# Output-projection pieces of a group-norm attention kernel regrouped: casts behind a block's last chain, stores and residual loads at a burst's head, chains of one tile evacuated together, last sums in two parts

## Chip, cores and metric

The kernel runs on one core of a Trainium2 chip. The metric is the device time of one execution in microseconds; it is compared by the median of several runs.

## What is computed

The input x has 4 batches of 512 channels with 48 x 48 = 2304 positions. Group normalisation over 32 groups is followed by a 1 x 1 convolution to q, k and v, attention in 8 heads of 64 channels over all 2304 positions, an output projection and the residual:

```
hn = group_norm(x, scale, bias)
qkv = einsum('oc,bct->bot', qkv_w, hn) + qkv_b          # 3 x 8 heads x 64, float16
w = softmax(einsum('bhct,bhcs->bhts', q*s, k*s))        # s = 64 ** -0.25
a = einsum('bhts,bhcs->bhct', w, v)
out = x + einsum('oc,bct->bot', proj_w, a) + proj_b
```

## The kernel before

**Tiling.** Channels lie in 4 chunks of 128 partitions, heads go in pairs, and the positions of queries are cut into 5 blocks: 0 to 3 of 512 columns, block 4 of 256. A *burst* is one step of the stream of attention work: three tiles `ps` of scores in PSUM (L924, a pair of heads side by side), three exponentials to `p` on ScalarE (L931), a running sum `acc` of them on VectorE (L978), and, two bursts later, three tiles' worth of products with v into `av` (L949). A full block takes 6 bursts, block 4 takes 3; with 16 pairs (4 batches x 4) there are 432 bursts. Scores, values and the opening's chains run in the pool `ps_s` (3 tiles of two PSUM banks each), `av` and the sums in `ps_av` (one bank), and all chains beside the stream in `ps_w` (one bank, `pw`).

**Beside the stream.** What the next pairs need is cut into pieces and put into a list `beside`: q and k chains (`qk_chain`, L709, evacuated by VectorE in L718), v chains (L754, L762), loading and normalising the next batch, and the output projection of the batch before. `fill(n)`, called once per burst, lets tasks run in a given room, raises a credit by the rate at which pieces come due (each piece has an estimated cost and a pair by which it must be done) and issues pieces from the head of the list as long as the credit is at least half of the piece's cost. Pieces have an earliest burst (`after`). A chain that starts is not joined by a second one in the same burst. The order on every engine is the order in which these Python calls are made; no scheduler changes it.

**Sums.** At a block's end `add_up` (L1000) multiplies `acc` with ones, VectorE copies the result (`slx`, L1013), SyncE's queue moves it (`sums<-slx`, L1016), VectorE inverts it (L1042), the queue writes it to memory and spreads it (`row<-inv` L1044, `ib<-row` L1054), and GpSimd multiplies (`att`, L1061). For the last two blocks, `divide_here` (L1020 to 1024) does it in place with a long reciprocal on VectorE.

**Output projection.** `att32` (L815 to 825) casts a block of `att` of up to four pairs on ScalarE to `a`; `proj_run` (L841) makes a chain of 8 matmuls (4 pairs, two parts of the weights, L831) in a bank; `evacuate` adds bias and residual on VectorE (L858, or L854 for a last part); `store` (L863) writes the result. `residual` (L793) loads the part of x to be added; its tiles `r` come from a pool of 4. `proj_piece` ties them together: it loads the residual of the next chain, makes its own chain, evacuates it, and puts the store into a list `loads` for the next burst. `do_tasks` (L1104), called by `fill`, runs what is due in `loads`, so stores and reloads stand in the middle of a burst, behind the block's sums and inversion. A cast is a piece of no cost, other small pieces cost 0.05.

**The last batch.** For blocks 2, 3 and 4 of the last batch the projection is made in two parts: `FIRST`, three pairs, during the last pair's bursts, and `LAST`, the last pair's own part, at the end. `ready` (L1130) tells how many bursts after a block's end its cast may stand. After the stream, the sums of the very last block are made in one go in the bank `pw` (36 matmuls), the sums are tested against limits (`fines`, `good`, `flag`), and the remaining chains run, each in a bank of `ps_s` of its own since `alone` is set again.

**The opening.** Before the stream, six chains (k of blocks 0 to 4, q of block 0) run side by side in the six banks of three `ps_s` tiles, channel chunk by channel chunk as the normalised chunks come; with the last chunk each is evacuated right after its own matmuls.

Of the kernel before, what the change touches and what calls it, by code (L numbers as in the profile page):

```python
# [12 lines left out]
F32 = mybir.dt.float32  # L13
# [13 lines left out]
P = 128  # L27
NC = C // P
# [5 lines left out]
BEHIND = 2  # L34
# [433 lines left out]
def fast_path(  # L468
# [226 lines left out]
    def qk_steps(g, part, j, bank=None):  # L695
        b, pr = divmod(g, NPAIR)
        o, n = QBLOCKS[j]
        pw = {0: bank}

        def one(c):  # L700
            if g not in qk:
                qk[g] = [
                    qkp.tile([P, T], F16, tag=a, name=f"{a}_{g}") for a in ("q", "k")
                ]
            if c == 0 and bank is None:
                pw[0] = chain_bank(f"pqk_{g}_{part}_{j}")
            w0 = part * C + pr * P
            for lo in (0, D):
                nc.tensor.matmul(  # L709
                    pw[0][lo : lo + D, :n],  # L710
                    wqkv[:, c, w0 + lo : w0 + lo + D],
                    hn[b, c, j],
                    start=(c == 0),
                    stop=(c == NC - 1),
                )
            if c == NC - 1:
                col = part * NPAIR + pr
                nc.vector.tensor_scalar(  # L718
                    qk[g][part][:, o : o + n],
                    pw[0][:, :n],  # L720
                    bqkv[:, col : col + 1],
                    SCALE,
                    ALU.add,
                    ALU.mult,
                )

        return one

# [137 lines left out]

    def proj_piece(b, j, chunks, pairs=range(NC), ahead=None):
        def run():
            if ahead is not None:
                ahead()  # L870
            evacuate, store = proj_run(b, j, chunks, pairs)
            evacuate()
            if pairs != FIRST:

                loads.append((now[0] + 1, store))

        return piece(QB / 290.0 * len(pairs) / NC, run, True, True)

    def proj_pieces(b, j):

        def ahead(k):
            if k < len(proj_list) and not in_two(b, proj_list[k][0]):
                residual(b, *proj_list[k])

        def begin():
            att32(b, j, LAST if in_two(b, j) else range(NC))
            if j == 0:
                ahead(0)  # L890

        pairs = LAST if in_two(b, j) else range(NC)
        chains = [
            proj_piece(b, j, chunks, pairs, lambda k=k: ahead(k + 1))
            for k, (jj, chunks) in enumerate(proj_list)
            if jj == j
        ]
        return [piece(0.0, begin)], chains

    av, acc, pts, avx, sums, rowd, ibs = {}, {}, {}, {}, {}, {}, {}

    stream = []
# [76 lines left out]
                nc.vector.tensor_tensor(t[:, 0], t[:, 0], t[:, r], ALU.add)  # L981
            acc[g, j] = [t[:, :1]]

    def add_up(g, j, bank=None):

        o, n = QBLOCKS[j]
        per = QB // n
        sl = bank
        if bank is None:
            sl = ps_av.tile([P, QB], F32, tag="av", name=f"sl_{g}_{j}")  # L990
        steps = [
            (t, r, a)
            for t in acc.pop((g, j))
            for r in range(t.shape[1])
            for a in range(per)
        ]
        for i, (t, r, a) in enumerate(steps):
            for h in range(2):
                lo = h * D
                nc.tensor.matmul(  # L1000
                    sl[lo : lo + D, :n],
                    ones16,
                    t[:, r, h, a * n : (a + 1) * n],
                    start=(i == 0),
                    stop=(i == len(steps) - 1),
                )
        return sl

    def rows(g, j, sl):
# [92 lines left out]
        normed[b, j, c] = now[0]  # L1102

    def do_tasks(room):  # L1104
        n = now[0]
        while loads and loads[0][0] <= n:
            loads.popleft()[1]()
        while tasks and tasks[0][0] <= n and room > 0:
            _, us, run = tasks.popleft()
            run()  # L1110
            room -= us
# [18 lines left out]
    def ready(b, j):  # L1130

        if b < B - 1:
            return BEHIND + 6
        return BEHIND + 5

    def put_convert(b, j):
        end = ends[((b + 1) * NPAIR - 1) * NQ + j]
# [16 lines left out]
    for b in range(B):  # L1154
# [20 lines left out]
        if b == B - 1:  # L1175
            put_qk(g + 3, 1)
            put_qk(g + 3, 0, range(NQ - 1))
            put_convert(old, 0)
            put_qk(g + 3, 0, (NQ - 1,))

            ahead = [
                (residual, b, j, chunks)
                for j in (NQ - 2, NQ - 3, NQ - 1)
                for jj, chunks in proj_list
                if jj == j
            ]
            for j in range(NQ):
                put_proj(old, j, ahead)
                if j + 1 < NQ:
                    put_convert(old, j + 1)  # L1190
                if j >= NQ - 2:

                    there = ends[(NG - 2) * NQ + j] + BEHIND + 6
                    put_run(att32, b, j, FIRST, after=there)
            put_first(b, NQ - 2)
            put_run(att32, b, NQ - 3, FIRST)
            put_first(b, NQ - 3)
            put_convert(b, 0)
            put_proj(b, 0)
            put_first(b, NQ - 1)  # L1200
            put_convert(b, 1)
            put_proj(b, 1)
            put_convert(b, NQ - 3)
            put_proj(b, NQ - 3)
            continue
# [38 lines left out]
    for c in range(NC):  # L1244

        for j in range(NQ):
            if j == 2:
                coefficients(0, (c,))
                norm_chunk(0, c)
            if c + 1 < NC:  # L1250
                stats(0, j, c + 1)
        if c + 1 < NC:
            aggregate(0, (c + 1,))
            group_scale(0, (c + 1,))
        for chain in chains:
            chain(c)
    for j in range(1, NQ):
        for p in qk_chain(0, 0, j):
            p[1]()
# [12 lines left out]
    def fill(n):  # L1272
# [1 line left out]

        now[0] = n
        idle = beside and beside[0][4] and not beside[0][4]()
        if ended(n - 1):
            room = 1.1 if idle else 0.0  # L1280
# [5 lines left out]
        rate, work = 0.0, 0.0  # L1286
        for us, _, _, _, _, _, need in beside:
            work += us
            left = min(need * per_pair, len(stream) - BEHIND) - n
            rate = max(rate, work / max(left, 1))  # L1290
        credit[0] = min(credit[0] + rate, 4.0)
        closed = False
        while beside:
            us, _, first, last, when, after, _ = beside[0]
            if after > n or (first and closed) or (when and not when()):
                break
            if credit[0] < us / 2:
                break
            issue()
            closed = closed or last  # L1300
# [19 lines left out]
        return stream[n][:2] if ended(n) and n not in soon else None  # L1320

    for n in range(end):
        summed = block_at(n - BEHIND - 1)
        if summed:
            rows(*summed, add_up(*summed))
# [34 lines left out]
        loads.popleft()[1]()  # L1360
    check_sums(g, NQ - 2)
    att32(b, NQ - 2, LAST)
    add(stream[-1])
    values(stream[-1])
    sl = add_up(g, j, small_bank("sl_last"))

    every = fine.shape[1] + n
    fines = work.tile([P, QB], F32, tag="rows", name="fines")[:, :every]
# [5 lines left out]
    nc.gpsimd.tensor_copy(fines[:, n:], fine)  # L1374
    divide_here(g, j, sl, av[0], nc.vector)
    att32(b, j, LAST)
    alone[0] = True
    while beside or loads:
        while loads:
            loads.popleft()[1]()  # L1380
# [75 lines left out]
```

## Time and profile before

| | us |
|---|---|
| median of 3 runs (lowest, highest) | 1635.6 (1634.31, 1636.46) |
| the profiled execution: its own time | 1636.04 |
| its span from first to last instruction | 1634.3 |
| TensorE matmul busy | 1586.6 |
| ScalarE busy | 1284.2 |
| VectorE busy | 1135.6 |
| GpSimd busy | 301.2 |
| idle before the first matmul | 12.3 |

The mean granted clock of TensorE is 0.996 of full speed. In the profile, engines are called PE (matmuls), PEld (weight loads), DVE (VectorE), ACT (ScalarE), POOL (GpSimd) and SP (the SyncE queue that issues nearly all DMAs). A name such as `pr<-a,whi` is output and inputs of an instruction, L831 its line in the listing above. In lists of waits the numbers are the total, how often, and the longest, in us. In a timeline a bracket tells how long the engine was idle ahead of the row and what ended that. Matmuls overlap: the end of each is modelled, so a gap is read from one end to the next start, while the pace is read from start to start.

### The profile page before, as it was taken

To read this page: it belongs to the slowest core of one execution; us is meant where nothing else is said; L and a number is where in the kernel's file an instruction comes from. 1 tells how busy PE (TensorE), PEld (TensorE's weight loads), DVE (VectorE), ACT (ScalarE), POOL (GpSimd) and SP (SyncE) were. 2 spreads that over 40 slices of the span, in tenths; PEclk is the share of its full clock that TensorE was granted. 3 is DMA by queue.
4 is the path that set the end of the run, shared out by engine and by line. 5 is a ranking of instruction groups with operands and counts; after the bars stand their busy time and mean duration, and the time that the engine had idled before them with its cause. 6 is when DMAs were issued, how large, how long until landed. Compare 5 with 4: busy or idle time off the path is not lost.

```text
span 1634.3 us, 28292 instructions
## 1 busy us (share of the span) xinstructions
PE 1586.6 (97%) x11500; PEld 696.5 (43%) x11500; DVE 1135.6 (69%) x1302; ACT 1284.2 (79%) x1398; POOL 301.2 (18%) x419
## 2 busy tenths in 40 slices
PE   6999999999999999999999999999999999999896
PEld 2533434443333534555333353455433334435444
DVE  6268668866676677886666667788666766666575
ACT  3077777888888888888887888897888888887784
POOL 1001112211121221212111121221211121211111
PEclk9999999999999999999999999999999999999999
DMA  6002021000000024511000001451100000015423
GB/s 219 1 14 64 13 59 28 18 14 11 14 18 14 15 62 130 140 47 37 14 13 13 14 18 39 140 154 43 37 14 17 15 11 14 18 40 174 114 72 119
DMA packets 94898, 82.11 MB, mean 50 GB/s; under 512 B 50852, under 2 KB 60964, under 8 KB 94756
## 3 DMA queue, kind: packets, MB, share of 16 engines
q1 hardware_dynamic: 92724, 78.35, 17.3%
q8 instruction: 92, 1.51, 0.4%
q10 hardware_dynamic: 1904, 1.84, 0.4%
q14 instruction: 50, 0.41, 0.1%
q0 software_dynamic: 128, 0.01, 0.0%
HBM read 60.70 MB, written 19.17 MB: 49 GB/s over the span
## 4 chain that ended last, share of the span: by engine, by line
PE 88%; DVE 4%; ACT 3%; DMA 3%; issue 1%; SPq 0%; DVEq 0%; ACTq 0%
PE pqk L709 29%; PE ps L924 18%; PE av L949 18%; PE pv L754 15%; PE pr L831 5%; ACT p L931 3%; DMA r<-x_dram 2%; PE ps L709 1%; DVE acc L978 1%; PE sl L1000 1%; DVE r L858 1%; ACT a L825 1%; DMA x<-x_dram 1%; DVE inv L1023 0%; DVE r L854 0%
## 5 line engine op out<-in xcount | busy, mean ns | idle before, releaser
L931 ACT ACTIVATE p<-ps 128x1024 f16<-128x1024 f32 x1296 | 1232.4, 1026 | 316.1 <-PE ps L924 315.5
L978 DVE TENSOR_TENSOR acc<-acc,p 128x3072 f16<-128x3072 f16 x270 | 482.8, 1788 | 71.0 <-ACT p L931 69.9
L709 PE MATMUL pqk<-x,wqkv 128*64 128x512 f32 (+1 forms) x2464 | 519.5, 551 | 0.5 <-DVE r L858 0.5
L924 PE MATMUL ps<-q,k 64*128 64x512 f16 (+1 forms) x2880 | 358.7, 358 | 5.9 <-ACT p L931 5.1
L949 PE MATMUL av<-p,v 128*64 128x512 f16 (+1 forms) x2880 | 361.5, 364 | 0.4 <-DVE slx L1013 0.3
L754 PE MATMUL pv<-wqkv,x 128*64 128x256 f32 x2304 | 268.8, 380 | 0.0
L709 PEld LDWEIGHTS pqk<-x,wqkv 128*64 128x64 f32 x2464 | 168.9, 137 | 224.5 <-issue 164.9
L1035 POOL TENSOR_SCALAR in<-sums 128x8 f32<-128x8 f32 (+1 forms) x158 | 110.5, 700 | 800.9 <-DMA sums<-slx 794.5
L924 PEld LDWEIGHTS <-k 64*128 64x128 f16 x2880 | 106.8, 94 | 285.5 <-issue 237.8
L949 PEld LDWEIGHTS <-v 128*64 128x64 f16 x2880 | 132.1, 109 | 212.0 <-issue 167.9
L1061 POOL TENSOR_TENSOR att<-avx,ib 128x512 f16<-128x512 f32 (+1 forms) x78 | 128.7, 1650 | 453.7 <-DMA ib<-row 404.1
L754 PEld LDWEIGHTS pv<-wqkv,x 128*64 128x64 f32 x2304 | 160.6, 137 | 92.4 <-DVE v L762 3.6
L978 DVE TENSOR_TENSOR acc<-p,p 128x3072 f16<-128x3072 f16 x79 | 139.8, 1770 | 0.0
L831 PE MATMUL pr<-a,whi 128*128 128x512 f32 (+1 forms) x312 | 123.5, 403 | 13.8 <-ACT a L825 7.3
L831 PE MATMUL pr<-a,wlo 128*128 128x512 f32 (+1 forms) x312 | 115.8, 377 | 0.0
L981 DVE TENSOR_TENSOR acc<-acc 128x1024 f16<-128x1024 f16 x156 | 109.3, 701 | 5.3
L718 DVE TENSOR_SCALAR q<-pqk,bqkv 128x512 f16<-128x512 f32 (+1 forms) x79 | 55.0, 696 | 83.6 <-PE pqk L709 83.2
L762 DVE TENSOR_TENSOR v<-pv,bv 128x512 f16<-128x512 f32 x72 | 49.8, 691 | 85.5 <-PE pv L754 85.3
L718 DVE TENSOR_SCALAR k<-pqk,bqkv 128x512 f16<-128x512 f32 (+1 forms) x75 | 52.2, 696 | 79.2 <-PE pqk L709 79.0
L858 DVE SCALAR_TENSOR_TENSOR r<-pr,bproj,r 128x512 f32<-128x512 f32 (+1 forms) x80 | 54.9, 695 | 65.7 <-PE pr L831 46.7
L958 DVE COPY avx<-av 128x512 f32<-128x512 f32 (+1 forms) x79 | 50.7, 641 | 65.2 <-PE av L949 65.0
L831 PEld LDWEIGHTS pr<-a,whi 128*128 128x128 f32 x312 | 59.1, 189 | 52.4 <-issue 15.4
(62 smaller groups left out, 448.7 us busy)
## 6 DMA issues: line engine op xcount, KB each, us to landing
r<-x_dram SPq DMA_DIRECT2D x72, 256.0 KB, 3.4
out_dram<-r SPq DMA_DIRECT2D x69, 256.0 KB, 2.3
ib<-row SPq DMA_DIRECT2D x126, 128.0 KB, 3.0
x<-x_dram SPq DMA_DIRECT2D x62, 256.0 KB, 4.2
x<-x_dram SPq DMA_DIRECT2D x16, 128.0 KB, 3.8
sums<-slx SPq DMA_DIRECT2D x128, 2.0 KB, 2.1
ib<-row SPq DMA_DIRECT2D x30, 64.0 KB, 2.9
wqkv<-qkv_wT_dram SPq DMA_DIRECT2D x2, 768.0 KB, 6.9
```

Of the source, the lines that this page charges most:

```text
L709: nc.tensor.matmul(pw[0][lo : lo + D, :n], wqkv[:, c, w0 + lo : w0 + lo + D], hn[b, c, j], start=(c == 0), stop=(c == NC - 1),)
L718: nc.vector.tensor_scalar(qk[g][part][:, o : o + n], pw[0][:, :n], bqkv[:, col : col + 1], SCALE, ALU.add, ALU.mult,)
L754: nc.tensor.matmul(pw[0][lo : lo + D, a, :], hn[b, c, i * P // QB][:, at + lo : at + lo + D], wqkv[:, c, 2 * C + half * C // 2 :][:, : C / ...
L831: nc.tensor.matmul(ps[:, :n], w[:, c, bass.ts(m, P)], at32[b, j, c], start=(i == 0), stop=(i == len(steps) - 1),)
L858: nc.vector.scalar_tensor_tensor(xt[:, i], places[i], bias, xt[:, i], ALU.add, ALU.add)
L924: nc.tensor.matmul(ps[:, h, a * n : (a + 1) * n], kt[rows, bass.ts(i, P)], qt[rows, o : o + n], start=True, stop=True,)
L931: nc.scalar.activation(pt[:, r], ps, AF.Exp)
L949: nc.tensor.matmul(av[0][lo : lo + D, :n], vv[b, pr // 2][:, i, pr % 2 * P + lo : pr % 2 * P + lo + D], pt[:, r, h, a * n : (a + 1) * n], ...
L978: nc.vector.tensor_tensor(t, before, pt, ALU.add)
L981: nc.vector.tensor_tensor(t[:, 0], t[:, 0], t[:, r], ALU.add)
L1035: nc.gpsimd.tensor_scalar(t, sm, limit, None, op)
L1061: nc.gpsimd.tensor_tensor(atts[g][:, o : o + n], avx.pop((g, j))[:, :n], ibs.pop((g, j))[:, :n], ALU.mult,)
```

## The change

1. `qk_steps` returns its evacuation where a bank is given; the opening evacuates chains by twos, after both halves of a tile are written.
2. `proj_piece` makes its chain first and puts both its store and the residual load of the chain after the next into `loads`; the first two residuals are loaded with the block's cast. `loads` is now run at the head of each burst, ahead of the sums and scores, no longer in `do_tasks`.
3. A piece of cost up to 0.1 is issued whatever the credit, so a cast follows right behind the chain before it.
4. The last batch's order of FIRST parts and casts is rewritten; the cast of block 2's LAST part may stand one burst earlier; the rate towards the end of the stream is reckoned to 4 bursts before the end instead of 2.
5. The last sums are made in two parts in a `ps_s` tile, the first before the last values; `alone` is not set again, so chains left over after the stream share `pw`.

```diff
@@ qk_steps
-            if c == NC - 1:
+            def evacuate():
                 col = part * NPAIR + pr
                 nc.vector.tensor_scalar(
...
+            if bank is not None:
+                return evacuate
+            if c == NC - 1:
+                evacuate()
@@ proj_piece
         def run():
-            if ahead is not None:
-                ahead()
             evacuate, store = proj_run(b, j, chunks, pairs)
             evacuate()
             if pairs != FIRST:
                 loads.append((now[0] + 1, store))
+            if ahead is not None:
+                loads.append((now[0] + 1, ahead))
@@ proj_pieces
             if j == 0:
                 ahead(0)
+                ahead(1)
...
-            proj_piece(b, j, chunks, pairs, lambda k=k: ahead(k + 1))
+            proj_piece(b, j, chunks, pairs, lambda k=k: ahead(k + 2))
@@ add_up
-    def add_up(g, j, bank=None):
+    def add_up(g, j, bank=None, more=False):
...
-                    start=(i == 0),
-                    stop=(i == len(steps) - 1),
+                    start=(i == 0 and (g, j) not in open_sums),
+                    stop=(i == len(steps) - 1 and not more),
                 )
+        if more:
+            acc[g, j] = []
+            open_sums.add((g, j))
@@ do_tasks
-        n = now[0]
-        while loads and loads[0][0] <= n:
-            loads.popleft()[1]()
-        while tasks and tasks[0][0] <= n and room > 0:
+        while tasks and tasks[0][0] <= now[0] and room > 0:
@@ ready
-        return BEHIND + 5
+        return BEHIND + (4 if j == NQ - 3 else 5)
@@ the last batch
-                if j >= NQ - 2:
-                    there = ends[(NG - 2) * NQ + j] + BEHIND + 6
-                    put_run(att32, b, j, FIRST, after=there)
-            put_first(b, NQ - 2)
-            put_run(att32, b, NQ - 3, FIRST)
-            put_first(b, NQ - 3)
+            for j in (NQ - 2, NQ - 3, NQ - 1):
+                there = ends[(NG - 2) * NQ + j] + BEHIND + 6
+                put_run(att32, b, j, FIRST, after=there)
+                put_first(b, j)
             put_convert(b, 0)
             put_proj(b, 0)
-            put_first(b, NQ - 1)
@@ the opening
-        for chain in chains:
-            chain(c)
+        for i, chain in enumerate(chains):
+            evacuate = chain(c)
+            if c == NC - 1 and i % 2 == 1:
+                before()
+                evacuate()
+            before = evacuate
@@ fill
-            left = min(need * per_pair, len(stream) - BEHIND) - n
+            left = min(need * per_pair, len(stream) - 4) - n
...
-            if credit[0] < us / 2:
+            if us > 0.1 and credit[0] < us / 2:
@@ the stream
     for n in range(end):
+        now[0] = n
+        while loads and loads[0][0] <= n:
+            loads.popleft()[1]()
@@ the end
     att32(b, NQ - 2, LAST)
+    sl = ps_s.tile([P, 2, QB], F32, tag="ps", name="sl_last")[:, 0, :]
+    add_up(g, j, sl, more=True)
     add(stream[-1])
     values(stream[-1])
-    sl = add_up(g, j, small_bank("sl_last"))
+    add_up(g, j, sl)
...
-    alone[0] = True
```

More of the change, by code (lines that the diff above doesn't have):

```diff
@@ L898, in proj_pieces @@
         return [piece(0.0, begin)], chains
+    open_sums = set()
     av, acc, pts, avx, sums, rowd, ibs = {}, {}, {}, {}, {}, {}, {}
@@ L1272, in fill @@
     def fill(n):
-        now[0] = n
         idle = beside and beside[0][4] and not beside[0][4]()
```

## The prediction

> **What bounds the kernel now.** I read the page first: busy shares, the slices, the chain that ended last. TensorE (PE) is busy almost throughout, and the change leaves every matmul in place, so only time in which PE waits, or runs slowed, can be won. The first line gives busy time, share and instructions per engine.
>
> ```profile
> PE 1586.6 (97%) x11500; PEld 696.5 (43%) x11500; DVE 1135.6 (69%) x1302; ACT 1284.2 (79%) x1398; POOL 301.2 (18%) x419
> ```
>
> So 1634.3 - 1586.6 = 47.7 us without a matmul: 12.3 before the first, 8.7 after the last, and gaps between. The waits of PE name what ended each gap (total, times, longest):
>
> ```profile
> PE pr L831 <- ACT a L825: 7.3, 3, 3.0
> PE pr L831 <- DVE r L858: 6.1, 8, 1.7
> PE ps L924 <- ACT p L931: 5.1, 12, 0.5
> PE ps L709 <- DVE k L718: 2.7, 3, 0.9
> ```
>
> All four are places that the diff touches: output chains (L831) waiting for the converted att (L825) or for the previous chain's evacuation (L858), scores (L924) waiting for exponentials (L931), and the opening chains (L709) waiting for evacuations (L718). In the PE timeline of the opening the bracket is idle time ahead of a row:
>
> ```profile
> 27.81 1.88 PE L709 MATMUL ps<-x,wqkv 128*64 128x512 f32 x8
> 30.64 1.94 PE L709 MATMUL ps<-x,wqkv 128*64 128x512 f32 x8 [0.95 <-DVE k L718]
> 33.52 1.51 PE L709 MATMUL ps<-x,wqkv 128*64 128x512 f32 x8 [0.94 <-DVE k L718]
> 35.83 1.08 PE L709 MATMUL ps<-x,wqkv 128*64 128x512 f32 x4 [0.80 <-DVE k L718]
> 36.74 1.46 PE L709 MATMUL pqk<-x,wqkv 128*64 128x512 f32 x6
> ```
>
> Last the chain of waits in the last batch (start, duration, what): the path leaves PE for ACT's casts, and the chain of 8 matmuls after that takes 3.63 and 2.85 us where its neighbours take 2.07.
>
> ```profile
> 1498.08 0.47 ACT p L931
> 1498.55 0.45 issue
> 1499.00 1.94 ACT p L931 x2
> 1500.94 0.51 ACT a L825
> 1501.45 0.04 issue
> 1501.49 3.63 PE pr L831 x8
> ...
> 1517.11 2.85 ACT p L931 x3
> 1519.97 0.51 ACT a L825
> 1520.48 0.04 issue
> 1520.53 2.85 PE pr L831 x8
> ...
> 1530.17 2.07 PE pr L831 x8
> ```
>
> [...] the table by windows has PEclk 0.66 at 1500 to 1505 us and 0.69 at 1520 to 1525, after idle gaps of 2.25 and 3.02 us[...]. [...] the exponentials of the next burst stand behind the four casts (2.18 us). [...] residual loads land 3.4 us after issue in the median, 6.15 at worst, and start late where SP stands at a wait.
>
> **The change part by part.** The 432 bursts, counted from 0, are my clock, from first score matmul to the next burst's. In the PE timeline a burst with a full output chain takes 3.59 us (scores 0.75, values 0.77, chain 2.07), with a partial chain of three pairs 3.12, and 0.34 more where a block's sums are added. What a burst takes beyond that I call its loss. Which chain, cast and load falls into which burst is the order in which the built programs' instructions stand.
>
> *Opening chains, evacuated by tiles.* Chains 0 and 1 write the two halves of one tile, and the wait is for the tile: chain 1 stands until chain 0 is evacuated. Afterwards all six run through, and DVE evacuates two at a time behind them. At the free pace, two column halves start each 0.43 us, so 512 columns take 0.86 and 256 take 0.43: 5 x 0.86 + 0.43 = 4.73 us. The row at 27.81 holds two pairs for the chain before and, from 28.67, chain 0's last part; so the chain after the sixth starts at 33.4 instead of 36.74: **3.3 us**. ACT's last normalisation (ends 30.34) is in time for the fourth chain (31.2); the evacuations (0.75 each) hide behind the following 3.43 us chains. PE is the bound from here to burst 155, so nothing gives the gain back.
>
> *Residual loads two chains ahead, with stores at the burst's head.* Batch 0's output stage (bursts 155 to 191) loses 5.7 us, batch 1's (271 to 290) 4.2. Of these, evacuations that stood for a residual load cost 1.66 (burst 164: load issued 659.82, DVE free from 661.84, went on at 664.32), 1.74 (burst 276), 0.63 of burst 167, about 0.5 together in 159 and 160, 0.5 in 191 and 0.18 in 277. Before, a load has one burst of lead and goes to SP behind that burst's row<-inv and ib<-row; afterwards two bursts, some 7 us, ahead of both. Worst landing 6.15, so these go: 5.2 us. Next late is DVE itself: in bursts 165 to 169 it carries 1.75 of adding, 0.75 of evacuation and 1.0 to 1.6 of normalisation in 3.59 us, and the group scale (2.5 with its aggregate) now meets a PE that no longer waits. I give back 0.7. **4.5 us**, of 3.0 to 5.5. Moved past on SP: a store (0.34) and a load (0.43 to 0.58) now stand ahead of a block's sums<-slx. The store waits for the evacuation, which ends 0.7 before slx, so the sums leave some 0.2 to 0.9 later. DVE's inv has stood 0.7 to 3.3 us behind the sums' landing: hidden.
>
> *Conversions right behind the last chain.* A conversion of no cost needed credit that the chain had just spent, so it slid into the next burst, right ahead of the chain that reads it. Losses in the last stage (outputs of batches 2 and 3): bursts 395: 1.23; 400: 0.54; 402: 0.68; 403: 3.82; 406: 0.17; 407: 4.46; 408: 0.27; 411: 2.35 (seven casts); 415: 0.32; 418: 0.95; 422: 1.01; 428: 0.99: 16.8 us. Afterwards each conversion is issued one burst ahead of its chain. It still costs: four casts push ACT 2.2 behind, a burst leaves it 3.59 - 2.85 = 0.74 to catch up, and scores wait for a free tile. That price stands in the same list, where the cast already went ahead: 1.23 for the first, behind q and k chains; 0.54 in steady bursts (400; 0.53 twice in batch 1); about 0.2 where a sum lengthens the burst; 1.0 behind the short partial chains. New conversions: 1.23 + 0.2 + 2 x 0.54 + 0.1 (half width) + 0.2 + 0.95 + 0.3 + 1.0 + 0.54 = 5.6. The 0.68 of 402 is a load wait (lead as above) and goes. 16.8 - 5.6 = 11.2, of which I count **10.5**, range 7 to 12, since a lag of ACT can meet the next one. Two casts come earlier against their inputs: block 2 of the last pair is cast one burst earlier, but POOL has it at 1600.58 and the cast could start at about 1606; block 1's is ready 11 us ahead.
>
> *Last sums in two parts, no separate banks at the end.* The 36 matmuls (2.15 us) waited until 1616.28 for the single bank pw. Now 24 run ahead of the last values, in another tile, and the last 12 end about 1.0 earlier; but ACT copies fines behind the cast of block 3 (which hung on inv, 3.35, and att), so the second inv starts only 0.8 earlier. Against that, the last two full-block chains share pw: the second waits until DVE, behind inv and att, has evacuated the first, a bubble of about 0.75, and one partial chain (0.55) has moved ahead of the last burst while one evacuation (0.63) left DVE's tail. 0.8 + 0.63 - 0.75 - 0.55 = **0.1**, between -1.2 (bubble on a slowed clock) and +1.5.
>
> *The rate towards the end (4 bursts instead of 2)* moves chains earlier and adds none: 0, hidden by PE being full; without that cover, one chain, 2 us.
>
> Sum: 3.3 + 4.5 + 10.5 + 0.1 = 18.4 us off the profiled execution, whose own time is 1636.04 (span 1634.3): 1617.6. The median of the three runs, 1635.6, stands 0.4 lower: **1617.2**.
>
> **Rivals.**
> A, *DVE and ACT become the bound of the output stages.* For: DVE is at 3.5 of 3.59 us in bursts 165 to 169, and ACT has only 0.74 spare. Against: the price of a cast is measured where it already went ahead. Loads then give 3.0, conversions 7, tail -1.2: 12.1 off, 1623.5.
> B, *all stalls go.* Loads 5.5, conversions 12, tail 1.5, opening 3.3: 22.3 off, 1613.3. For: the slowed clock (1.57 + 0.78 + 0.3 us of stretched chains) surely disappears. Against: each cast delays exponentials wherever it stands.
> C, *slower: the block's sums stand behind the stores on SP.* The store waits on DVE, sums<-slx behind it on SP, inv in DVE's order waits for the sums, the chain's evacuation behind inv, PE for the bank. Eleven block ends lie in store-carrying bursts. Their slack is about 2.2 us on average, and a delay shows from 0.7; to turn an 18.4 gain into 3.3 lost (0.2%), each must lose 21.7 / 11 = 2.0 beyond it, a delay of 4.2. I find at most 0.9. Time 1639.
> D, *it doesn't do what it says*: casts stay next to their readers and only the opening is won: 1632. The order of instructions excludes most of it.
>
> **Chances.** Forecast 0.58, A 0.20, B 0.14, C 0.05, D 0.03. Measurement tells about 0.2% (3.3 us) from no change: faster 0.92, same 0.03, slower 0.05. The forecast's own band, 1615 to 1621, widened to A and B: 1612.5 to 1624.5.
>
> **What would show it.** Right: no wait of PE for L718 in the opening and q chains from 33.4 us; PE's wait for casts near zero before the tail, no window of PEclk under 0.9 between 1450 and 1600; waits for exponentials still some 5 us; no DVE wait for r<-x_dram. Wrong: PE's wait for DVE r above 5 us, inv waiting for sums, or a tail (last burst's start to the end) longer than 22.9 us.

## The result and the profile after

| | before | after |
|---|---|---|
| median of 4 runs each (lowest, highest), us | 1636.03 (1634.31, 1637.38) | 1618.38 (1617.16, 1619.89) |
| ratio after / before, 95% interval | | 0.9893 [0.9876, 0.991] |
| the profiled execution: own time / span | 1636.04 / 1634.3 | 1618.91 / 1617.1 |
| idle of PE within the span | 47.7 | 33.7 |
| matmul busy | 1586.6 | 1583.4 |

The change is faster by 17.65 us (1636.03 - 1618.38); the forecast was 18.4 less and a time of 1617.2. The spans differ by 17.2: 14.0 less idle (47.7 - 33.7), and 3.2 less busy time with the same 11500 matmuls. First the page, busy time per engine:

```profile
PE 1583.4 (98%) x11500; PEld 695.5 (43%) x11500; DVE 1136.2 (70%) x1302; ACT 1282.8 (79%) x1398; POOL 298.4 (18%) x419
```

The other engines' counts and times are almost as before; the work only stands elsewhere. PE's waits (total, times, longest):

```profile
...
PE ps L932 <- ACT p L939: 5.3, 12, 0.5
PE pr L837 <- DVE r L860: 3.2, 1, 3.2
PE pr L837 <- DVE q L719: 1.3, 1, 1.3
...
PE pr L837 <- DVE r L864: 0.2, 1, 0.2
```

(The first row left out is the wait for the first input. The lines have moved: L837 is the chain, L831 the cast, L864 its evacuation, L932 the scores.) The wait for casts, 7.3 us before, is not in the list; that for steady evacuations went from 6.1 to 0.2; the opening's wait for L718 is gone. What stays is the wait for exponentials, 5.3 in 12 pieces, in size as forecast; 3.0 of it, in 6 pieces, lies in the last stage, and not all of that comes from casts (see below). Two are new: 3.2 in the tail, and 1.3 behind a q evacuation.

The opening in PE's timeline is now one row without a bracket inside, and the next chain follows it:

```profile
12.83 21.98 PE L709 MATMUL ps<-x,wqkv 128*64 128x512 f32 x96 [12.83 <-ACT x L667]
34.64 1.88 PE L709 MATMUL pqk<-x,wqkv 128*64 128x512 f32 x8
```

The chain of waits in the last batch, at the place where two casts of before had held up PE:

```profile
1486.12 2.86 ACT p L939 x3
1488.98 0.42 ACT a L831
1489.48 0.40 issue
1490.40 0.64 ACT a L831
1491.04 2.77 ACT p L939 x3
1494.24 0.77 PE av L957 x6
1495.01 2.07 PE pr L837 x8
```

The cast is still on the path, but as ACT's own delay ahead of exponentials; the chain behind it takes 2.07 and no longer 3.63 or 2.85. The table by windows shows the clock there (in order: length, busy time and number of instructions of PE, PEld, DVE, ACT and POOL; PEclk; DMA share; GB/s):

```profile
1500.00:1505.00 5.00, 5.00 (x46) 3.00 (x44) 4.40 (x7) 4.26 (x6) 2.73 (x4) 1.00 0.46 143
...
1520.00:1525.00 5.00, 5.00 (x41) 3.10 (x38) 3.78 (x5) 4.64 (x7) 0.91 (x1) 1.00 0.53 146
```

PEclk is 1.00 where it was 0.66 and 0.69. The forecast put the matmuls stretched by the slowed clock at 1.57 + 0.78 + 0.3 = 2.65 us, which would be the greater part of the 3.2 us less busy time.

**By stage.** From the first score matmul of each burst, spans of stretches of bursts in us. All other kernels are in the table too; the sections below use it. *Opening* is chain 0's last part to the chain after the sixth.

| kernel | opening | 154-191 | 262-309 | 310-393 | 394-412 | 413-430 | last burst to end | span |
|---|---|---|---|---|---|---|---|---|
| before | 8.07 | 141.27 | 176.13 | 279.97 | 82.76 | 65.76 | 22.89 | 1634.3 |
| after | 4.72 | 137.46 | 175.19 | 284.60 | 69.47 | 64.18 | 22.77 | 1617.1 |
| opening alone | 4.72 | 143.14 | 176.69 | 279.83 | 81.17 | 65.73 | 23.05 | 1632.8 |
| casts alone | 8.07 | 142.11 | 177.85 | 279.82 | 74.80 | 65.42 | 22.98 | 1629.8 |
| loads alone | 8.07 | 138.19 | 175.33 | 279.82 | 83.12 | 65.75 | 23.15 | 1631.8 |
| after, all in mid-burst | 4.72 | 140.65 | 175.92 | 284.59 | 74.56 | 64.16 | 22.75 | 1624.9 |
| after, one residual ahead | 4.72 | 146.44 | 188.90 | 284.59 | 83.93 | 70.41 | 23.90 | 1661.6 |
| after, reloads in mid-burst | 4.72 | 137.44 | 174.16 | 284.60 | 69.44 | 64.18 | 22.69 | 1615.2 |
| after, own banks | 4.72 | 137.47 | 175.13 | 284.60 | 69.43 | 64.18 | 21.49 | 1615.0 |
| after, sums in one go, own banks | 4.72 | 137.44 | 175.23 | 284.60 | 69.41 | 64.16 | 22.24 | 1615.1 |
| after, casts spread | 4.72 | 137.46 | 175.53 | 283.62 | 68.69 | 62.52 | 24.08 | 1613.8 |
| after, rate as before | 4.72 | 137.43 | 175.05 | 279.83 | 71.51 | 65.16 | 26.23 | 1617.2 |
| after, again | 4.72 | 137.46 | 175.35 | 284.60 | 69.54 | 64.19 | 24.14 | 1617.4 |
| three repairs together | 4.72 | 137.47 | 174.15 | 283.62 | 68.77 | 62.54 | 21.47 | 1610.5 |

Bursts 0 to 153 (545.29 to 545.65) and 192 to 261 (240.30 to 240.31) are equal in all.

### The profile page after: what moved, and what is told of

Its sections match the earlier page's. It is cut to its first block, busy times and chain, and to the rows that moved or that the text cites. A ratio compares the mean times of both kernels' runs of the same rounds, so it can differ in the third digit from the quotient of the medians.

```text
span 1617.1 us, 28315 instructions
## 1 busy us (share of the span) xinstructions
PE 1583.4 (98%) x11500; PEld 695.5 (43%) x11500; DVE 1136.2 (70%) x1302; ACT 1282.8 (79%) x1398; POOL 298.4 (18%) x419
## 4 chain that ended last, share of the span: by engine, by line
PE 91%; ACT 4%; issue 2%; DVE 1%; DMA 1%; POOL 0%; SPq 0%; ACTq 0%; DVEq 0%; POOLq 0%
PE pqk L709 29%; PE ps L932 19%; PE av L957 19%; PE pv L760 16%; PE pr L837 7%; ACT p L939 3%; PE ps L709 1%; PE sl L1009 1%; ACT a L831 1%; DMA x<-x_dram 1%; DVE acc L986 0%; DMA sums<-slx 0%; DVE r L860 0%; DMA row<-inv 0%; DMA ib<-row 0%
## 5 line engine op out<-in xcount | busy, mean ns | idle before, releaser
L932 PE MATMUL ps<-q,k 64*128 64x512 f16 (+1 forms) x2880 | 359.5, 358 | 6.2 <-ACT p L939 5.3
L1047 POOL TENSOR_SCALAR in<-sums 128x8 f32<-128x8 f32 (+1 forms) x158 | 116.6, 738 | 795.0 <-DMA sums<-slx 788.7
L932 PEld LDWEIGHTS <-k 64*128 64x128 f16 x2880 | 107.3, 94 | 286.1 <-issue 238.1
L1073 POOL TENSOR_TENSOR att<-avx,ib 128x512 f16<-128x512 f32 (+1 forms) x78 | 120.0, 1539 | 450.4 <-DMA ib<-row 406.3
L837 PE MATMUL pr<-a,whi 128*128 128x512 f32 (+1 forms) x312 | 122.2, 399 | 4.6 <-DVE r L860 3.2
L837 PE MATMUL pr<-a,wlo 128*128 128x512 f32 (+1 forms) x312 | 114.4, 373 | 0.0
L719 DVE TENSOR_SCALAR q<-pqk,bqkv 128x512 f16<-128x512 f32 (+1 forms) x79 | 55.0, 696 | 80.4 <-PE pqk L709 79.8
L719 DVE TENSOR_SCALAR k<-pqk,bqkv 128x512 f16<-128x512 f32 (+1 forms) x75 | 52.2, 696 | 78.1 <-PE pqk L709 78.0
L864 DVE SCALAR_TENSOR_TENSOR r<-pr,bproj,r 128x512 f32<-128x512 f32 (+1 forms) x80 | 54.9, 694 | 43.6 <-PE pr L837 43.0
L837 PEld LDWEIGHTS pr<-a,whi 128*128 128x128 f32 x312 | 58.5, 187 | 41.9 <-issue 18.7
```

Of the source, the lines that this page charges most:

```text
L719: nc.vector.tensor_scalar(qk[g][part][:, o : o + n], pw[0][:, :n], bqkv[:, col : col + 1], SCALE, ALU.add, ALU.mult,)
L837: nc.tensor.matmul(ps[:, :n], w[:, c, bass.ts(m, P)], at32[b, j, c], start=(i == 0), stop=(i == len(steps) - 1),)
L864: nc.vector.scalar_tensor_tensor(xt[:, i], places[i], bias, xt[:, i], ALU.add, ALU.add)
L932: nc.tensor.matmul(ps[:, h, a * n : (a + 1) * n], kt[rows, bass.ts(i, P)], qt[rows, o : o + n], start=True, stop=True,)
L1047: nc.gpsimd.tensor_scalar(t, sm, limit, None, op)
L1073: nc.gpsimd.tensor_tensor(atts[g][:, o : o + n], avx.pop((g, j))[:, :n], ibs.pop((g, j))[:, :n], ALU.mult,)
```

## Experiments

The runs came in three groups, each on one chip with its own runs of before, whose medians are 1638.49, 1639.89 and 1637.49. Times are compared within a group. Place by place, the stages above are the sharper measure: each comes from a single profile, but they repeat in several kernels.

**Opening alone.** Only item 1 of the change, on the kernel before.

```diff
+                return evacuate            # in qk_steps, where a bank is given
+            if c == NC - 1 and i % 2 == 1:  # in the opening
+                before()
+                evacuate()
```

> The kernel before with the paired evacuation of the opening chains alone. Theory (PE stands for a whole tile, and is the bound from there to burst 155): from the start of chain 0's last part to the first following chain 4.7 us instead of 8.07, and the whole kernel 3.3 us faster, some 1632.5, with the later stages as before. Rival (the gain is given back at a later wait, for the v weights or the first scores): the first burst starts where it did and the time stays within 1 us of 1635.8.

Measured: 1635.11 against 1638.49, ratio 0.9982 [0.9971, 0.9992]. The opening went from 8.07 to 4.72, 3.35 us, in this and every other kernel that has the edit. The rest of this kernel is that of before, and yet its stage 154-191 is 1.87 us longer. The difference is in its waits of DVE for residuals: 17.5 us in 11, against 10.9 in 5 in the profile of before. So the loads of before cost a different amount in these two executions, and the one profile that was read had a low one.

**Casts alone.** Only the rule for pieces of no cost, on the kernel before.

```diff
-            if credit[0] < us / 2:
+            if us > 0.1 and credit[0] < us / 2:
```

> The kernel before with the credit rule alone: pieces of cost up to 0.1 are issued whatever the credit. Theory (casts next to their readers are what costs, and the clock slows behind these gaps): PE's wait for ACT a falls from 7.3 us to about 0, no window under 0.9 of the clock in the last stage, bursts 394 to 431 8 to 10 us shorter, 1626 to 1628 in all. Rival (the rewritten order and the earlier rate are needed for it): under 4 us, above 1631. A third, that the casts' price comes back as waits for exponentials: these grow from 5 to over 10 us.

Measured: 1630.07 against 1638.49, ratio 0.9945 [0.9929, 0.9962]. PE's wait for casts falls from 7.3 to 0.2, and that for exponentials stays at 4.9, so the rise to over 10 of the third theory does not come. In 394-412 the edit wins 7.96 us: bursts 403 and 407 go from 7.75 and 8.05 to 3.93 and 5.11, burst 411 from 5.94 to 3.63. But burst 407 keeps 1.5 us, and 410 and 412 rise by 1.18 and 0.85. What stands there is in DVE's timeline:

```profile
1513.64 0.42 DVE L958 COPY avx<-av 128x256 f32<-128x256 f32 x1 [0.85 <-PE av L949]
1517.26 0.75 DVE L858 SCALAR_TENSOR_TENSOR r<-pr,bproj,r 128x512 f32<-128x512 f32 x1 [3.20 <-DMA r<-x_dram]
```

An evacuation waits 3.20 us for its residual. Where the chain stood for a cast before, the load had time to land. Taking away one wait uncovered the other.

**Loads alone.** Item 2, on the kernel before.

```diff
+            if ahead is not None:
+                loads.append((now[0] + 1, ahead))
...
-            proj_piece(b, j, chunks, pairs, lambda k=k: ahead(k + 1))
+            proj_piece(b, j, chunks, pairs, lambda k=k: ahead(k + 2))
...
+        while loads and loads[0][0] <= n:   # at the head of a burst
+            loads.popleft()[1]()
```

> The kernel before with the loads alone: chain first, stores and residual loads at the burst's head, two residuals ahead. Theory: bursts 154 to 192 3 to 4 us shorter, 262 to 310 1 to 2, the last stage 0.5 to 1; 1630 to 1631.5. If x reloads ahead of the sums are what made PE wait 1.3 us at burst 274, that wait comes here too. Rival (it is DVE that is late, not the loads): under 1.5 us.

Measured: 1631.38 against 1638.49, ratio 0.9959 [0.9945, 0.9973]. Stages 154-191 and 262-309 win 3.08 and 0.80 and DVE's list has no wait for a residual any more. In 394-412 nothing is won (83.12 for 82.76): there the casts cover the loads. Burst 274 takes 4.76 here instead of 3.58, and inv waits 2.0 us for its sums, which comes back below.

So in 394-412 the parts do not add. Casts alone -7.96, loads alone +0.36, together 7.6; the kernel that has both with the planner's rate of before (below) has 11.25 less there. The remaining 3.65 us appears only with both edits; that kernel also has the rewritten order of the last batch and the earlier cast of block 2, which were not run by themselves. This interaction rests on single profiles of one stretch. In medians of whole runs the opening, the casts and the loads alone are 3.38, 8.42 and 7.11 us below before, 18.9 in all against 17.65 for the change, each of the three uncertain by some 2 to 3 us: the loads are worth more there than in the stages, which fits the few waits for residuals in the profile of before (10.9 us, against 17.5 and 18.0 in these runs' opening alone and casts alone).

**Two ahead, but in mid-burst.** The changed kernel, with stores, residuals and reloads run by `do_tasks` again.

```diff
-        while loads and loads[0][0] <= n:   # at the head of a burst
-            loads.popleft()[1]()
+        while loads and loads[0][0] <= n:   # in do_tasks, as before
+            loads.popleft()[1]()
```

> The changed kernel with stores, loads and reloads run in the middle of a burst again, as before, but still two residuals ahead. Theory (the lead is what counts, not the head): within 1 us of the changed kernel's 1618.4, and the wait of DVE for the sums at burst 274 is gone, since the x loads stand behind the sums: 1617 to 1618. Rival (the head of the burst is what counts): the waits of evacuations for residual loads come back, 2 us or more slower, above 1620.5.

Measured: 1625.16 against 1638.49, ratio 0.9913 [0.9897, 0.993], against 0.9893 [0.9876, 0.991] for the changed kernel. The span is 7.8 longer than after's, and DVE waits for residuals again, 17.9 us in 9. The theory that the lead of two chains is what counts, and the place not, falls. SP's queue of this kernel around burst 407 shows why:

```profile
1503.44 0.43 SPq L810 DMA_DIRECT2D r<-x_dram  x1
1507.41 0.38 SPq L1056 DMA_DIRECT2D row<-inv  x1
1507.88 0.42 SPq L869 DMA_DIRECT2D out_dram<-r  x1
1508.34 0.43 SPq L810 DMA_DIRECT2D r<-x_dram  x1
```

and its DVE:

```profile
1505.85 1.42 DVE L989 TENSOR_TENSOR acc<-acc 128x1024 f16<-128x1024 f16 x2
1507.19 0.20 DVE L1054 RECIPROCAL inv<-sums 128x8 f32<-128x8 f32 x1
...
1513.80 0.75 DVE L864 SCALAR_TENSOR_TENSOR r<-pr,bproj,r 128x512 f32<-128x512 f32 x1 [4.01 <-DMA r<-x_dram]
```

In mid-burst the load stands behind `row<-inv`. It left SP after row, although the store's evacuation ahead of it had long ended; row waits for inv, and inv stands on DVE behind two additions and an evacuation. SP stood from 1503.87 to 1507.41, the load left at 1508.34 and landed by 1513.80, when DVE had stood 4.01 us for it. At the head of the burst the same load stands ahead of row and leaves as soon as the store's evacuation is done: in after the store goes at 1501.06, the load at 1501.50 and row at 1504.29.

**One ahead, at the head.** The changed kernel, with one residual ahead of its chain instead of two.

```diff
-                ahead(1)
...
-            proj_piece(b, j, chunks, pairs, lambda k=k: ahead(k + 2))
+            proj_piece(b, j, chunks, pairs, lambda k=k: ahead(k + 1))
```

> The changed kernel, but a chain orders the residual of the next chain instead of the one after it (one residual with the block's cast instead of two); loads and stores stay at the head of a burst. With the run that kept two ahead but stood in the middle of a burst this tells place from lead. Theory (both are needed: the head alone puts the load after the store of the chain before): the load is issued some 0.4 us behind the end of an evacuation and lands 3.4 later, where the next evacuation would start 2.8 behind that end: about 1.0 us lost per chain that follows another in the next burst, some 20 to 45 of them, waits of PE for DVE r above 20 us, median 1637 to 1665. Rival (the head of a burst is all that counts, the second residual ahead is idle): 1617 to 1620.

Measured: 1663.80 against 1637.49, ratio 1.0177 [1.015, 1.0203]. The theory named first holds, near the upper end of its numbers. The list of DVE's waits:

```profile
DVE r L864 <- DMA r<-x_dram: 51.5, 30, 4.0
```

and of PE's:

```profile
PE pr L837 <- DVE r L864: 28.3, 32, 2.2
```

30 evacuations wait for their load, 1.7 us on average, and PE for them. So neither half of item 2 does it alone: place without lead loses 45 us against after on one chip (1663.80 - 1619.15), lead without place 7.8 in span.

**Reloads of x back in mid-burst.** The changed kernel; only the reloads of x (`load_block`) leave the list that runs at the head.

```diff
-        loads.append((now[0] + 1, run))
+        reloads.append((now[0] + 1, run))   # run by do_tasks
```

> The changed kernel with only the reloads of x back in the middle of a burst, behind the block's sums; stores and residual loads stay at the head. Theory (four x loads ahead of sums<-slx make DVE's inv wait 2.2 us at burst 272, and PE 1.3 us): that wait is gone, bursts 262 to 310 take 1.3 us less than 175.2, the rest as the changed kernel; about 1617. Rival (a late landing by chance, or DVE's other work): it stays.

Measured: 1616.87 against 1639.89, ratio 0.9864 [0.9833, 0.9895]; span 1615.2. It tests where the wait of 1.3 for L719 in the list after comes from. Burst 274 takes 4.94 there. DVE in the changed kernel:

```profile
1040.49 1.76 DVE L986 TENSOR_TENSOR acc<-acc,p 128x3072 f16<-128x3072 f16 x1 [1.09 <-ACT p L939]
1044.41 0.18 DVE L1054 RECIPROCAL inv<-sums 128x4 f32<-128x4 f32 x1 [2.17 <-DMA sums<-slx]
```

and SP's queue:

```profile
1035.59 1.67 SPq L810 DMA_DIRECT2D r<-x_dram  x2
1037.37 1.80 SPq L512 DMA_DIRECT2D x<-x_dram  x4
1039.26 1.14 SPq L1028 DMA_DIRECT2D sums<-slx  x2
```

Four reloads (1.80 us of issuing) now stand ahead of the block's sums. The sums leave late and land slowly, 5.15 us after their issue (1039.26 to 1044.41), where 2.1 is the median; inv waits 2.17 us for them, the q evacuation behind inv frees the bank late, and PE stands 1.28. With the reloads back behind the sums, the same queue reads:

```profile
1037.61 1.14 SPq L1028 DMA_DIRECT2D sums<-slx  x2
1038.85 1.96 SPq L512 DMA_DIRECT2D x<-x_dram  x4
```

Inv comes at 1041.75 without a wait, burst 274 takes 3.58, PE's wait is gone, and stage 262-309 is 1.03 shorter, less than the 1.3 expected, since burst 268 takes 0.34 more. This is the mechanism of rival C, with reloads in place of the stores, and at one place instead of eleven.

**Own banks at the end.** The changed kernel with `alone` set again after the stream.

```diff
     att32(b, j, LAST)
+    alone[0] = True
```

> The changed kernel with a bank of its own for each chain left over at the end (alone set again). Theory (the shared bank makes PE stand 3.2 us, but DVE's row of evacuations bounds the tail): PE's long gap moves, the last burst to the end 22.77 becomes 22.0 to 22.7. Rival (the bank is the bound): 2 to 3 us shorter, 20 to 21.

Measured: 1616.81 against 1639.89, ratio 0.9861 [0.9831, 0.9892]; span 1615.0. The last burst to the end takes 21.49 instead of 22.77, which lies between the two ranges expected: the bank costs more than the theory said and less than the rival.

**Sums in one go, own banks.** The changed kernel with the tail of before.

```diff
-    sl = ps_s.tile([P, 2, QB], F32, tag="ps", name="sl_last")[:, 0, :]
-    add_up(g, j, sl, more=True)
...
-    add_up(g, j, sl)
+    sl = add_up(g, j, small_bank("sl_last"))
...
+    alone[0] = True
```

> The changed kernel with the tail as before: the last sums in one go in the bank pw, own banks for the chains left. Theory (the two parts win 0.8 at the second inv, the shared bank gives most of it back): the last burst takes 22.6 to 23.6, within 1 us of the changed kernel. Rival (the two-part sum is worth its 1.5 us of matmuls): 24.2 or more.

Measured: 1617.14 against 1639.89, ratio 0.9862 [0.9831, 0.9893]. The tail takes 22.24, a little under the range of the theory. With own banks, the sums in two parts are therefore worth 22.24 - 21.49 = 0.75 us.

**The changed kernel again,** beside the last group.

> The changed kernel as it is, once more, beside the others on one chip. Expected: a ratio to the kernel before of 0.9893 within its interval of 0.9876 to 0.991; a span of 1615.5 to 1617.5, the difference lying ahead of the first burst, and burst 274 again near 4.9 us. If burst 274 is back at 3.6 here, the wait behind the reloads was an accident of one execution.

Measured: 1619.15 against 1637.49, ratio 0.9888 [0.9872, 0.9905]; burst 274 takes 5.10, so that wait is no accident. The span, 1617.4, is as expected, but not for the reason given: ahead of the first burst 1.3 us are less indeed (it starts at 76.52 instead of 77.84), and the tail takes 1.4 more, 24.14 for 22.77. PE's timeline in the tail of the first profile after:

```profile
1600.36 0.40 PE L837 MATMUL pr<-a,wlo 128*128 128x512 f32 x1
1603.94 0.50 PE L837 MATMUL pr<-a,whi 128*128 128x512 f32 x1 [3.19 <-DVE r L860]
...
1604.74 0.40 PE L837 MATMUL rest<-a,wlo 128*128 128x512 f32 x1
1604.98 0.39 PE L837 MATMUL rest<-a,whi 128*128 128x512 f32 x1
```

and of this one:

```profile
1602.85 0.50 PE L837 MATMUL pr<-a,whi 128*128 128x512 f32 x1 [3.21 <-DVE r L860]
...
1603.82 0.63 PE L837 MATMUL rest<-a,wlo 128*128 128x512 f32 x1
1604.24 0.63 PE L837 MATMUL rest<-a,whi 128*128 128x512 f32 x1
```

The stand is the same, 3.19 and 3.21: the second chain in `pw` waits for the first one's evacuation. But afterwards matmuls of 512 columns start every 0.24 us in the first (1604.74 to 1604.98) and every 0.42 in the second (1603.82 to 1604.24), where the granted clock was 0.50. The shared bank so costs 1.28 or 24.14 - 21.49 = 2.65 us, by whether the clock falls.

**Rate as before.** The changed kernel with the planner's rate reckoned to two bursts before the end.

```diff
-            left = min(need * per_pair, len(stream) - 4) - n
+            left = min(need * per_pair, len(stream) - BEHIND) - n
```

> The changed kernel with the planner's rate towards the end reckoned to two bursts before the end of the stream, as before the change. Theory (the rate moves chains and adds none; PE is full): within 0.15% of the changed kernel, 1615 to 1619.5, stages before burst 310 unchanged, single bursts of the last stage differing in both directions. Rival (the earlier end is worth a chain that would otherwise be left over behind the stream, or the burst without a chain at 395 comes from it): a last burst 2 us longer, or bursts 393 to 397 some 2 us shorter.

Measured: 1619.36 against 1637.49, ratio 0.9891 [0.9875, 0.9907]; the changed kernel on the same chip 1619.15. As forecast, nothing in the whole; but by stage two differences cancel. The tail is 26.23, 2.1 longer than that of the changed kernel run beside it, also slowed: one more chain of two matmuls is left over behind the stream, and it waits 0.79 for the shared bank. This half of the rival is there. The stages 310 to 430 are 1.75 shorter (416.50 for 418.25), some 0.55 of it these two matmuls. The other half of the rival is there only in kind: burst 395 takes 4.81 and 396 3.59, where the changed kernel has 1.52, without any chain beside the stream, and 4.97, so the empty burst does come from the rate; but bursts 393 to 397 take 18.82 in both kernels, because in the changed kernel they hold less work: q and k chains of theirs run earlier, in bursts 363 and 389.

**Casts spread.** The changed kernel; in the last stage two of a block's four casts go one burst each ahead, into a second set of tiles taken from x's. A second set of all four casts was not tried.

```diff
+    for p in [p for p in beside if id(p) in casts_of]:
...
+            beside.insert(i + 1, piece(0.0, lambda cast=cast: att32(*cast)))
```

> The changed kernel with the casts of the last stage spread: two pairs of a block are cast one per burst ahead (in two tiles of x that are free by then), the other two behind the last chain. Theory (four casts at once put ACT 2.2 us behind and a burst gives back 0.74; two put it 1.1 behind, which the tiles of scores absorb): PE's waits for exponentials in bursts 386 to 431 go from about 3.3 us to under 1, and that stage is 2 to 4 us shorter; 1614.5 to 1616.5. Rival (ACT simply has that much work, and the waits come back elsewhere): the stage stays within 1 us.

Measured: 1615.77 against 1639.89, ratio 0.9855 [0.9823, 0.9886]. The stages 310 to 430 are 3.42 shorter (414.83 for 418.25): bursts 393, 403, 417 and 423 take 3.59, 3.93, 3.25 and 3.79 instead of 4.57, 4.48, 4.14 and 4.41. PE's waits for exponentials fall from 5.3 in 12 to

```profile
PE ps L944 <- ACT p L951: 3.4, 8, 0.5
```

In the last stage 1.0 in 2 is left of 3.0 in 6, both in burst 396, which still takes 4.97. So ACT's delay by four casts in a row was 3.4 us of the price that stayed, and burst 396 is something else (see the account below). The tail gave 1.3 back to the slowed clock (24.08).

**Three repairs together.** Reloads in mid-burst, own banks, casts spread.

> The changed kernel with the three repairs that the single runs pointed to, together: reloads of x back in the middle of a burst, own banks for the chains left at the end, and the last stage's casts spread over bursts. Theory (three separate mechanisms at separate places): the gains add. Reloads 1.0 us (burst 274 at 3.6 instead of 4.94), own banks 1.3 (last burst 21.5 instead of 22.8), spread casts 3.4 (bursts 310 to 431), and the span of the changed kernel's profile held about 1 us of late opening: span 1610.5, median 1611 to 1613, no wait of PE for DVE r over 1 us at the end and none for inv of burst 274. Rival (the waits share their slack, what is won at one place is given back at the next): half of it, 1614 to 1615, with new waits of PE in the list.

Measured: 1612.32 against 1637.49, ratio 0.985 [0.9836, 0.9864], and 6.83 less than the changed kernel on the same chip (1619.15). The span is 1610.5, as the sum of the three said. The gains add, since they lie at separate places. This is the fastest kernel of the study. Its largest wait of PE after the opening's is that for exponentials, 3.4; then:

```profile
PE rest L845 <- DVE inv L1047: 1.7, 1, 1.7
```

## Why the prediction was right

| term | forecast | measured in the stages |
|---|---|---|
| opening | 3.3 | 8.07 - 4.72 = 3.35 |
| loads | 4.5 | 3.81 + 0.94 = 4.75 |
| conversions | 10.5 | 428.49 - 418.25 = 10.24 (bursts 310 to 430) |
| tail | 0.1 | 22.89 - 22.77 = 0.12 |
| rate | 0 | 0.2 in the median, two differences of about 2 that cancel |

The sum of the stages is 18.5, the span won 17.2. The 1.25 between them lie ahead of the opening's last chunk, which came at 29.92 instead of 28.67; the kernels with this opening have it anywhere from 28.43 to 29.92, and those without at 28.67 to 29.55, so the edit does not show in it.

*Opening.* Right in mechanism and size: pace times columns gave 4.73 us, and 4.72 was measured in every kernel with the edit, since all six chains run at PE's own pace.

*Loads.* The stalls that were listed went, all of them. The step "Moved past on SP: a store (0.34) and a load (0.43 to 0.58) now stand ahead of a block's sums" was incomplete: the reloads of x pass through the same list, four DMAs of 1.80 us. That cost 1.36 at burst 274 (4.94 for 3.58), a loss which the forecast had as "hidden"; "inv waiting for sums" was one of its own signs of being wrong, and it came, with 2.17 us. With the reloads back, the two stages win 3.83 + 1.97 = 5.8, more than the forecast's 5.2 less 0.7: DVE gave back less than was set aside for it. The forecast also took the stalls of one execution as the kernel's; the waits for residuals were 10.9, 17.5 and 18.0 us in three executions with the same policy of loading.

*Conversions.* The total is near, the casts' waits and the slowed stretches are gone as said, and a price stays; but the parts are not those of the forecast. First, the 10.24 belongs to the casts and the loads together. With the cast rule alone the stages 310 to 430 win 428.49 - 420.05 = 8.44, with the loads in mid-burst again 428.49 - 423.31 = 5.18: casts and loads had covered each other, and that they are separate terms holds only where both edits are made. Second, the price, forecast 5.6. The bursts above pace by 0.2 or more lose 5.9: 0.98 (393), 1.38 (396), 0.24 (397), 0.55 (403), 0.21 (407), 1.02 (417), 0.32 (421), 0.82 (423), 0.41 (425). But only 3.9 of it are casts (393, 403, 407, 417, 421, 423), the larger ones near what the forecast gave such a place (0.98 for 1.23, 0.55 for 0.54, 1.02 and 0.82 for 0.95 and 1.0). In 397 PE waits 0.2 for a residual, in 425 0.3 for `slx`. And 396 is the empty burst: in 395 PE has 1.52 us of work and ACT 2.85, so PE stands in 396 until ACT is done, with no cast in bursts 394 to 396. Without the new rate this loss is gone, and with the casts spread it stays. The forecast had it at nothing, "hidden by PE being full". That 5.6 and 5.9 agree is luck: the casts cost 1.7 less, and what was left out makes up for it.

*Tail.* That 0.1 meets 0.12 is luck too. The forecast's sum, 0.8 + 0.63 - 0.75 - 0.55, counts the partial chain of 0.55 that moved ahead of the last burst; in the table that chain lies in the stages 310 to 430, so the forecast to compare with 0.12 is 0.68. Measured: sums in two parts 0.75 (forecast 0.8); the work that left the tail 22.89 - 22.24 = 0.65 (forecast 0.63); the shared bank 22.77 - 21.49 = 1.28 (forecast 0.75). Here the bank was mis-sized: PE stands 3.2 for it, of which the rest chains would have stood 1.7 for inv in any case. Where the clock falls, the bank costs 2.65, and the tail is 24.14, longer than the 22.9 that the forecast named as a sign of being wrong; this is its lower bound, "-1.2 (bubble on a slowed clock)", as 24.14 - 22.89 = 1.25.

*Rivals.* A put loads at 3.0, conversions at 7 and the tail at -1.2; only the tail is seen, in some executions. B's "all stalls go" is refuted by 5.3 us of waits for exponentials. C's mechanism exists, but behind the reloads and not the stores, and its size is 1.36. D is refuted by the opening alone, 0.9982 [0.9971, 0.9992], against 0.9893 for the whole.

## What to carry to other kernels

A DMA's lead is counted from where the issuing queue can reach it, not from where the program orders it (in mid-burst SP stood from 1503.87 to 1507.41 for `row<-inv`, the load behind it left at 1508.34, and DVE stood 4.01 us for it): before raising a lead, look for an instruction ahead of it on the queue that waits for an engine, and when loads are moved ahead, list every DMA that passes through the same list (here four reloads, 1.80 us on SP, ahead of sums for which inv then waited 2.17). Stalls that cover one another (here a cast and a load at the same chain) do not add: the loads alone were worth nothing in 394-412 and 3.65 us more with the casts moved, so the credit goes by the order in which they are removed. A planner that shifts work by a burst or two can win nothing in the whole and still leave an empty burst and a shorter tail that cancel; read it by stage. And when a total comes out as forecast, compare the parts on the same borders: two of the terms here were right only in sum.

## What was not expected of the hardware

A stand of PE of about 3.2 us slowed the clock in some executions and not in others: 3.19 did not (after, and two ahead but in mid-burst), nor 3.21 (reloads in mid-burst); 3.20 (casts spread) and 3.21 (after again, rate as before) did, and then 512 columns took 0.42 instead of 0.24. In the profiles of before and after again the granted clock changes at times that lie multiples of 3.41 us apart: 1501.42, 1504.83, 1521.90, 1525.31 and 1627.71 in before, 1603.44, 1606.85 and 1610.26 in after again. Cut into stretches of that length, counted back from a change of the clock (1603.44 in after again; after has one change, at 1612.65), the two profiles of the changed kernel differ. In the tables by windows the second number is PE's busy time, and PEclk stands third from the end. In the first profile the stand falls into two stretches, 1.66 (3.41 - 1.75) and 1.53 (3.42 - 1.89) without a matmul, and no clock is lost:

```profile
1599.00:1602.41 3.41, 1.75 (x22) 1.11 (x18) 1.46 (x2) 0.99 (x2) 2.93 (x7) 1.00 0.25 87
1602.41:1605.83 3.42, 1.89 (x8) 1.57 (x9) 2.32 (x5) 0.40 (x1) 1.45 (x3) 1.00 0.20 77
```

In the second 2.82 of it (3.41 - 0.59) falls into one, and the next stretch has half the clock:

```profile
1600.03:1603.44 3.41, 0.59 (x3) 0.51 (x4) 2.73 (x3) 0.40 (x1) 2.57 (x5) 1.00 0.02 8
1603.44:1606.85 3.41, 3.41 (x10) 2.67 (x9) 1.98 (x3) 0.00 (x0) 0.00 (x0) 0.50 0.41 154
```

So the slowed clock goes, in these traces, not with the length of a gap but with how much of it lies in one stretch, and the stretch needn't be idle throughout. In the profiles of before and after, the four stretches at full clock with the most time without a matmul (2.04, 2.17, 2.55 and 3.41 us) were each followed by half the clock, and none with 1.67 or less was. No threshold follows from it: in opening alone 1.65 (at 660 us) was followed by half the clock and 1.91 (at 1056 us) was not. In before, the gaps of 2.25 and 3.02 put 2.17 and 2.04 into one stretch, and the next one ran at 0.50; the third, 2.04, put 1.61 there, and the clock stayed at 1.00. The 3.2 us of the shared bank so cost the clock in one profile of the changed kernel and not in the other, by how they fell into the stretches; what sets where a stretch begins was not shown.

Where no load is waited for, time repeats closely: stage 154-191 took 137.43 to 137.47 in eight profiles, of the changed kernel and of its variants that keep its residuals and stores, against 141.27 to 143.14 in three with the loads of before.
